# Last chunk of a two-layer mixture-of-experts kernel: half of its experts scaled by ScalarE and summed by TensorE with an identity; 6 buffers for expert values and 5 for fetched ones

## The chip, the core and the metric

The kernel runs on one core of one Trainium2 chip. A core has a matrix engine (TensorE, PE in the profile), a vector engine (VectorE, DVE), a scalar engine (ScalarE, ACT), a general engine (GpSimd, POOL), which here mostly issues gathers, and SyncE (SP), which issues plain transfers. Each engine takes its instructions from its own queue, in order. The metric is the device time of one execution in microseconds (us), the median of several runs.

## What is computed

Input x is 4 x 1024 tokens of 256 numbers in float32. There are two layers; each adds a gated attention-like part and a gated mixture of 8 experts, of which every token uses the best 2. The change lies in the mixture of the second layer. Cut to what matters:

```python
logits = x @ router_w.T                       # 8 experts
probs = softmax(logits)
topk_vals, topk_idx = top_k(probs, 2)
topk_w = topk_vals / (topk_vals.sum(-1) + 1e-06)
expert_out = einsum('nh,eho->eno', x, expert_weights)   # 256 -> 256 for each expert
out = ((expert_out[topk] + probs[topk]) * topk_w).sum()
x = x + gb * out                              # gb: one row of 256 for each batch
```

## The kernel before, in words

The tokens are cut into 8 chunks (c = 0 to 7) of 4 batches x 128 tokens. Layer 0 fills the time up to about 640 us and is not touched. In layer 1 each chunk is normalised (`normal`), goes through a gated feed-forward part (`fast`), is normalised again, and is routed (`routed`, `shares`).

**Chunks 0 to 6 do the experts sparsely.** Chunks 0 to 3 form one group (`ga`), chunks 4 to 6 another (`gb`). The normalised rows of a group are stored to memory (`gb_rows`) and sorted by expert into blocks of 128: 39 blocks for `ga`, 31 for `gb`. For each block, `block` (L2142) fetches 128 rows with a gather on POOL (tile `xg`), transposes them on PE (L2176), copies them with ACT (`xT`, L2182), multiplies them by one expert's matrix on PE (`p_e`, L2193), copies the result with ACT from PE's accumulator into a buffer `y` (L2203), and stores it with SP to memory (`gb_y`, L2206). The room for `y` is 3 buffers. When all blocks of a group are stored, `combine` (L1408) fetches for each chunk and each batch the two values of every token: two gathers on POOL into one buffer `yg` (L330), whose room is 3 buffers (`yg2=3`), then one ACT instruction (L1433) and three of DVE (L1439, L1442, L1444), the last of which adds to the tokens `x_sb`. After four batches a chunk is stored by SP in one transfer of 512 KB (L2381). For `gb` there are 3 x 4 = 12 such combinations with 24 gathers.

**Chunk 7 does its experts densely** (`dense`, L2213), all 8 for all tokens, so that its routing needs no sorting. For each batch b and each pair of experts j (0 to 3), PE multiplies the batch's tokens by the pair's matrices (L2241; two matmuls into one buffer of 512 numbers, shown by the profile as 4 records), and DVE multiplies each half by the token's weight for this expert and adds it to a running sum (`step`; L2257 for expert 0, L2266 for the others). At the end of a batch `done` (L2284) multiplies the sum by the gate (L2286) and adds it to `x_sb` (L2287), and SP stores 128 KB (L2290). The buffer of a pair is one of 3 (`p1`); the running sums have 2 buffers (`step`).

**What sets the order.** The instructions of layer 1 are not written in their final order. Each piece of work is given to a planner (`class Plan`, L39) with its engine, an estimated cost in us, what it comes after, which buffers it holds (the room by kind stands in `room1`, L1373 on) and a rank. `run` (L61) plays the work through in its own time: whenever an engine is free, the ready piece with the lowest rank is begun if its buffers are free, and the order that comes out is what each engine's queue then holds. So a new room or a new cost can move any later piece. The ranks that matter here: blocks of `gb` 7.35 to 8.0 (L2352), combinations of `gb` from 7.89 on (L2377), dense matmuls 8.23 + 0.1 b + 0.02 j (L2271), DVE's work on their results 0.5 below that (L2280), `done` 8.23 + 0.1 b (L2292).

Of the kernel before, what the change touches and what calls it, by code (L numbers as in the profile page):

```python
# [12 lines left out]
ALU = mybir.AluOpType  # L13
# [6 lines left out]
P = 128  # L20
B, S, D = 4, 1024, 256
NC = S // P
KD = D // P
E = 8
# [113 lines left out]
def adaln_d2_kernel(  # L138
# [20 lines left out]
    nc = tc.nc  # L159
# [7 lines left out]
    ps_2 = ctx.enter_context(tc.tile_pool(name="ps_2", bufs=2, space=PSUM))  # L167
    ps_m = ctx.enter_context(tc.tile_pool(name="ps_m", bufs=3, space=PSUM))

    def psum(pool, shape, name):  # L170
        tag = {id(ps_1): "p1", id(ps_2): "p2", id(ps_m): "pm"}[id(pool)]
        t = pool.tile([P, 512], F32, tag=tag, name=name)
        n = 1
        for s in shape[1:]:
            n *= s
        v = t[: shape[0], :n]
        if len(shape) == 3:
            v = v.rearrange("p (a b) -> p a b", b=shape[2])
        return v
# [57 lines left out]
    ident = const.tile([P, P], F32, name="ident")  # L237
# [3 lines left out]
    rank = const.tile([P, E], F32, name="rank")  # L241
# [600 lines left out]
    plan = Plan(p1=3, p2=2, pm=3, xn1=5, h1T=2, xn2=6, h2T=2, t1=1)  # L842
    PE, ACT, DVE, POOL = "PE", "ACT", "DVE", "POOL"
# [397 lines left out]
    ps = plan.slot("p1")  # L1241
# [27 lines left out]
    for half in range(2):  # L1269
        ps = plan.slot("p1")  # L1270
# [11 lines left out]
        m = plan(PE, 0.3, turn, after=routes, holds=[ps], rank=rank_)  # L1282
# [6 lines left out]
    for piece in range(3):  # L1289
        ps = plan.slot("p2")  # L1290
        m = loaded
        for k in range(KD):
# [12 lines left out]
            m = plan(PE, 0.87, mm, after=[m, of_batch["routed"]], holds=[ps], rank=20.0)  # L1305
# [5 lines left out]
    ps = plan.slot("p1")  # L1311
    d = of_batch["turned"]
    m = plan(PE, 0.2, lambda: g0.total_staged(ps_1), after=[d], holds=[ps], rank=-1.0)
    ps2 = plan.slot("p1")

    def bases():
# [3 lines left out]
    d = plan(DVE, 3.9, lambda: g0.close_staged(pa), after=[m], holds=[ps], rank=-1.0)  # L1320
# [4 lines left out]
        after=[m2],  # L1325
        holds=[ps2],
        rank=-0.9,
    )
    ps = plan.slot("p1")
    m = plan(PE, 0.4, lambda: g0.across(ps_1), after=[d], holds=[ps], rank=-1.0)  # L1330
    kept_busy(1.1, [m], 30.0)
    d = plan(DVE, 1.4, lambda: g0.limits(pa), after=[m, bs], holds=[ps], rank=-1.0)
    plan(DVE, 1.2, lambda: g0.list_weights(pa), after=[d], holds=[ps], rank=-0.75)
    for j in range(AHEAD):
        ps = plan.slot("p1")
# [12 lines left out]
        m = plan(PE, 0.25, look, after=[r], holds=[ps], rank=first)  # L1348
# [20 lines left out]
    for j in range(g0.J - SPARE, g0.J):  # L1369
# [6 lines left out]
        p2=2,  # L1376
        pm=3,
        yg1=3,
        yg2=3,
        h1=2,  # L1380
        h2=2,
        hT1=2,
# [1 line left out]
        hf=10,  # L1384
        xg=4,
        xT=3,
        y=3,
        reached=3,
        diff=2,
        step=2,  # L1390
# [6 lines left out]
    made = {}  # L1397
    home = {"yg1": early, "h1": early, "hT1": early, "tiny": early}

    def buf(kind, shape):  # L1400
        return (home[kind] if kind in home else late).tile(
            shape, F32, tag=kind, name=kind, bufs=room1[kind]
        )

    def tiny(shape, tag, n=2, dt=F32):
        return home["tiny"].tile(shape, dt, tag=tag, name=tag, bufs=n)
# [279 lines left out]
    plan = Plan(rings=RINGS, **room1)  # L1686
# [178 lines left out]
    plan = Plan(rings=RINGS, **room1)  # L1865
# [199 lines left out]
    def shares(g, c, at, vb, x, rank):  # L2065

        key = ("m", c)

        def do():
            x = made[key, "x"]  # L2070
            down = tiny([P, B, E + 1], "rdown")
            nc.vector.tensor_scalar(down, x, -1.0, 1.0, ALU.mult, ALU.add)
            nc.vector.reciprocal(down, down)
            nc.vector.scalar_tensor_tensor(x, x, 1.0, down, ALU.add, ALU.mult)
            p = tiny([P, 2, B], "rp")
            nc.vector.tensor_reduce(p[:, 0, :], x[:, :, :E], AX.X, ALU.add)
            nc.vector.reciprocal(p[:, 0, :], p[:, 0, :])
            nc.vector.tensor_tensor(
                p[:, 1, :].unsqueeze(2), x[:, :, E : E + 1], p[:, 0, :].unsqueeze(2), ALU.mult
            )  # L2080
            total = tiny([P, B], "rtotal")
            nc.vector.scalar_tensor_tensor(
                total, p[:, 0, :], 1e-6, p[:, 1, :], ALU.add, ALU.add
            )
            nc.vector.reciprocal(total, total)
            w = g.w[:, :, at : at + B]
            nc.vector.tensor_tensor(
                w, p, total.unsqueeze(1).to_broadcast([P, 2, B]), ALU.mult
            )
            nc.vector.tensor_tensor(p, p, w, ALU.mult)  # L2090
            nc.vector.tensor_tensor(vb[:, at : at + B], p[:, 0, :], p[:, 1, :], ALU.add)

        return plan(DVE, 2.2, do, after=[x[0]], holds=[x[1]], rank=rank)
# [119 lines left out]
    def dense(c, slotT, ts, d, x, rank):  # L2213

        key = ("d", c)
        g = last_pairs
        vb = tiny([P, B], "d_vb", 1)
        x = shares(g, c, 0, vb, x, rank)

        def spread_w():  # L2220
            w = made[key, "w"] = tiny([P, B, E], "d_w", 1)
            v = tiny([P, B, E], "d_v", 1)
            for i, t in ((0, w), (1, v)):
                nc.vector.tensor_tensor(
                    t,
                    g.one[:, i, :, :],
                    g.w[:, i, :].unsqueeze(2).to_broadcast([P, B, E]),
                    ALU.mult,
                )
            nc.vector.tensor_tensor(w, w, v, ALU.add)  # L2230

        x = plan(DVE, 0.6, spread_w, after=[x, d], rank=rank)
        for b in range(B):
            last, st = [], plan.slot("step")
            for j in range(E // 2):
                ps = plan.slot("p1")

                def mm(b=b, j=j):
                    p1 = made[key, b, j] = psum(ps_1, [P, 2, D], "p1_e")
                    for k in range(KD):  # L2240
                        nc.tensor.matmul(  # L2241
                            p1,
                            lhsT=made["n2", c, "hT"][:, k, b, :],
                            rhs=ew[:, 2 * j : 2 * j + 2, k, :],
                            start=(k == 0),
                            stop=(k == KD - 1),
                        )

                def out_(b=b, j=j):
                    if j == 0:  # L2250
                        made[key, "sum", b] = tiny([P, D], "step")
                    w, sum_ = made[key, "w"], made[key, "sum", b]
                    for i in range(2):
                        e = 2 * j + i
                        p = made[key, b, j][:, i, :]
                        if e == 0:
                            nc.vector.tensor_scalar(  # L2257
                                sum_,
                                p,
                                w[:, b, e : e + 1],  # L2260
                                vb[:, b : b + 1],
                                ALU.mult,
                                ALU.add,
                            )
                        else:
                            nc.vector.scalar_tensor_tensor(  # L2266
                                sum_, p, w[:, b, e : e + 1], sum_, ALU.mult, ALU.add
                            )

                m = plan(  # L2270
                    PE, 1.74, mm, after=ts, holds=[ps, slotT], rank=rank + 0.1 * b + 0.02 * j  # L2271
                )
                last = [
                    plan(
                        DVE,
                        0.95,
                        out_,
                        after=[m, x, *last],
                        holds=[ps, st],
                        rank=rank + 0.1 * b + 0.02 * j - 0.5,  # L2280
                    )
                ]

            def done(b=b):  # L2284
                sum_, xs = made[key, "sum", b], x_sb[:, c, b, :]
                nc.vector.tensor_tensor(sum_, sum_, mods1[GB][:, b, :], ALU.mult)  # L2286
                nc.vector.tensor_tensor(xs, xs, sum_, ALU.add)  # L2287

            def store(b=b):
                nc.sync.dma_start(out[b, c * P : (c + 1) * P, :], x_sb[:, c, b, :])  # L2290

            f = plan(DVE, 0.9, done, after=last, holds=[st], rank=rank + 0.1 * b)  # L2292
            plan(SP, 0.1, store, after=[f], rank=rank)

    last_pairs = Pairs(l1, l1, "gc", B)
# [8 lines left out]
    for c in range(NC):  # L2304
# [26 lines left out]
        if c == NC - 1:  # L2331
            d, x = routed(last_pairs, c, 0, slotT, ts, 7.46)
            dense(c, slotT, ts, d, x, 8.23)
            continue
        g, first = groups[which], 4 * which
        at = (c - first) * B
        d, x = routed(g, c, at, slotT, ts, c + 1.05)
# [12 lines left out]
        if c in (3, 6):  # L2350
# [15 lines left out]
            for q in range(first, c + 1):  # L2366
                done = combine(
                    "c2",
                    q,
                    "yg2",  # L2370
                    y_of[which],
                    g,
                    lambda b, q=q, first=first: (q - first) * B + b,
                    vbs[which],
                    mods1[GB],
# [70 lines left out]
```

## Time and profile before

| what | us |
|---|---|
| median of 3 runs (1152.88 to 1153.03) | 1153.02 |
| profiled execution, its own time | 1154.62 |
| span of the profiled execution | 1152.6 |
| PE busy in the span | 1100.8 (96%) |
| DVE, ACT, POOL busy | 586.6, 425.1, 410.6 |
| first gather of the last 12 combinations begins (POOL) | 1109.01 |
| last DVE instruction begins | 1148.23 |

The profile is one execution seen from inside. A line of a timeline gives the start, the length, the engine, the line of the kernel, the operation with output and input tiles, the number of instructions, and in brackets how long the engine had been idle before and what released it. A line of the groups gives count, busy time, and mean duration in ns. "Granted clock" is the share of TensorE's clock that its throttle let through.

A table of the last stretches, from the view of busy time by stretch:

| stretch, us | PE | DVE | ACT | POOL | granted clock |
|---|---|---|---|---|---|
| 1080 to 1095 | 13.83 of 15 | 7.38 | 7.79 | 9.55 | 1.00 |
| 1095 to 1105 | 8.84 of 10 | 3.78 | 4.74 | 1.58 | 1.00 |
| 1105 to 1115 | 10.00 of 10 | 6.05 | 1.57 | 4.72 | 1.00 |
| 1115 to 1125 | 10.00 of 10 | 8.31 | 2.12 | 7.61 | 1.00 |
| 1125 to 1135 | 6.33 of 10 | 6.74 | 1.17 | 4.24 | 1.00 |
| 1135 to 1142 | 3.63 of 7 | 6.22 | 1.51 | 4.33 | 0.76 |

### The profile page before, as it was taken

What the parts mean: (1) busy time and instruction counts of PE and PEld (TensorE: products, weight loads), DVE (VectorE), ACT (ScalarE), POOL (GpSimd) and SP (SyncE); (2) the same over time, 40 slices, a digit from 0 to 9 for tenths busy, and PEclk for the clock granted to TensorE, in tenths of its full rate; (3) what the DMA queues carried; (4) which work ended last, traced back from release to release, by engine and by line L of the source; (5) the groups of instructions that cost most, each with busy time, mean ns of one, the idle gap of its engine ahead of it and who ended that gap; (6) DMA issues with size and microseconds to landing.
All of it is one profiled execution on the core that took longest, in us unless ns stands there. A gap on an engine that the chain in (4) does not pass through costs nothing. (4 is left out here: it accounts for less than half of the span.)

```text
span 1152.6 us, 18406 instructions
## 1 busy us (share of the span) xinstructions
PE 1100.8 (96%) x6236; PEld 872.3 (76%) x6236; DVE 586.6 (51%) x2245; ACT 425.1 (37%) x1148; POOL 410.6 (36%) x477
## 2 busy tenths in 40 slices
PE   8999999999999999999989989999999999999893
PEld 5996899999999999999978455675667676646751
DVE  7777233222222212222245589878587535787566
ACT  5975333233333323233324433423324325342421
POOL 1000444333443344333463452420124332644644
PEclk8999999999999999999998999999999999999997
DMA  9412514564522415151251211200013323342544
GB/s 320 163 54 92 178 50 147 192 220 151 188 78 75 156 33 193 37 188 38 74 197 46 66 55 52 62 29 18 1 38 104 112 71 97 102 127 86 147 108 130
DMA packets 79369, 123.18 MB, mean 107 GB/s; under 512 B 23646, under 2 KB 63076, under 8 KB 74668
## 3 DMA queue, kind: packets, MB, share of 16 engines
q0 software_dynamic: 31680, 69.61, 19.9%
q1 hardware_dynamic: 46492, 50.80, 13.3%
q10 hardware_dynamic: 1104, 1.58, 0.4%
q8 instruction: 52, 0.85, 0.3%
q14 instruction: 41, 0.34, 0.1%
HBM read 205.18 MB, written 30.58 MB: 205 GB/s over the span
## 5 line engine op out<-in xcount | busy, mean ns | idle before, releaser
L1599 ACT ACTIVATE hid<-p_h,w 128x128 f32<-128x128 f32 x544 | 155.1, 368 | 338.0 <-issue 257.1
L1587 PEld LDWEIGHTS p_h<-xT,w 128*128 128x128 f32 x2176 | 255.4, 193 | 7.8 <-DVE xT L1572 4.0
L1587 PE MATMUL p_h<-xT,w 128*128 128x128 f32 x2176 | 257.1, 277 | 3.8 <-DVE xT L1572 3.2
L1610 PE MATMUL p_y<-w,hid 128*128 128x256 f32 x1088 | 251.6, 384 | 3.2 <-issue 3.2
L1884 PE MATMUL p_u<-hT,a 128*128 128x512 f32 x512 | 230.7, 595 | 0.8 <-ACTq L1848 0.8
L330 POOL DMA_INDIRECT w<-in_W,g_wrow x134 | 133.7, 998 | 271.6 <-ACT hid L1599 129.9
L1610 PEld LDWEIGHTS p_y<-w,hid 128*128 128x128 f32 x1088 | 202.6, 191 | 29.2 <-issue 4.2
L1884 PEld LDWEIGHTS p_u<-hT,a 128*128 128x128 f32 x512 | 94.2, 190 | 97.2 <-issue 89.3
L1572 DVE COPY xT<-pm_x 128x256 f32<-128x256 f32 x68 | 28.8, 424 | 186.8 <-PE pm_x L1567 176.4
L1932 PE MATMUL p_f<-a,hf 128*128 128x256 f32 x512 | 116.8, 380 | 3.9 <-DVE ln_mv L1467 1.6
L1621 DVE TENSOR_TENSOR y<-p_y,w 128x256 f32<-128x256 f32 x68 | 28.8, 424 | 176.1 <-PE p_y L1610 176.1
L1932 PEld LDWEIGHTS p_f<-a,hf 128*128 128x128 f32 x512 | 95.9, 190 | 22.6 <-issue 5.7
L330 POOL DMA_INDIRECT xg<-h_rows,g_row x68 | 65.7, 966 | 123.7 <-DVE g_hits L734 103.3
L330 POOL DMA_INDIRECT yg<-y,g_slot x64 | 61.4, 959 | 86.7 <-DVE x_sb L1444 33.5
L2193 PE MATMUL p_e<-ew,xT 128*128 x280 | 70.4, 384 | 0.3 <-ACT y L2203 0.3
L330 POOL DMA_INDIRECT xg<-ga_rows,ga_row x39 | 37.2, 954 | 91.3 <-DVE ga_row L743 35.0
L1896 ACT ACTIVATE hf<-p_u,decay 128x512 f32<-128x512 f32 x56 | 38.0, 683 | 72.6 <-PE p_u L1884 68.5
L2193 PEld LDWEIGHTS p_e<-ew,xT 128*128 128x128 f32 x280 | 49.4, 190 | 10.6 <-issue 5.1
L1507 DVE TENSOR_TENSOR h<-h,mod 128x256 f32<-128x256 f32 x128 | 51.5, 425 | 9.2 <-ACT h L1497 6.3
L1900 DVE SCALAR_TENSOR_TENSOR hf<-p_u,decay,hf 128x512 f32<-128x512 f32 x56 | 41.9, 748 | 21.8 <-PE p_u L1884 14.5
L2203 ACT COPY y<-p_e 128x256 f32<-128x256 f32 x70 | 26.0, 371 | 57.1 <-PE p_e L2193 24.8
L1980 POOL TENSOR_TENSOR x_sb<-x_sb,step 128x256 f32<-128x256 f32 x32 | 23.7, 743 | 62.2 <-DVE step L1973 44.5
(363 smaller groups left out, 1283.6 us busy)
## 6 DMA issues: line engine op xcount, KB each, us to landing
y<-y SPq DMA_DIRECT2D x68, 128.0 KB
ga_y<-y SPq DMA_DIRECT2D x39, 128.0 KB
x_sb<-in_x SPq DMA_DIRECT2D x8, 512.0 KB
h_rows<-xn SPq DMA_DIRECT2D x8, 512.0 KB
gb_y<-y SPq DMA_DIRECT2D x31, 128.0 KB
out_x<-x_sb SPq DMA_DIRECT2D x7, 512.0 KB
a<-in_fw SPq DMA_DIRECT2D x6, 512.0 KB
mod<-mod_rows SPq DMA_DIRECT2D x6, 512.0 KB
```

Source lines behind the costliest of these rows:

```text
L330: return nc.gpsimd.indirect_dma_start(out=dst, out_offset=None, in_=table, in_offset=bass.IndirectOffsetOnAxis(ap=index, axis=0), bounds_c ...
L1507: nc.vector.tensor_tensor(h, h, mods1[(sc, sh)[i]][:, b, :], (ALU.mult, ALU.add)[i])
L1572: nc.vector.tensor_copy(xT, pt)
L1587: nc.tensor.matmul(p1[:, i, :], lhsT=w1[:, k * H + m * P : k * H + (m + 1) * P], rhs=xT[:, k, :], start=(k == 0), stop=(k == KD - 1),)
L1599: nc.scalar.activation(hid[:, m, :], p1[:, i, :], AF.Relu, bias=w1buf[j % 2][:, KD * H + m : KD * H + m + 1],)
L1610: nc.tensor.matmul(p2, lhsT=hid[:, m, :], rhs=w2[:, m * D : (m + 1) * D], start=(m == 0), stop=(m == KH - 1),)
L1621: nc.vector.tensor_tensor(y, p2, w2buf[j % 2][:, KH * D :], ALU.add)
L1884: nc.tensor.matmul(pu, lhsT=a[:, k, m * P : (m + 1) * P], rhs=made["n1", c, "hT"][:, k, :, :], start=(k == 0), stop=(k == KD - 1),)
L1896: nc.scalar.activation(made[key, m], made[key, m, 0], AF.Silu, scale=decays[c])
L1900: nc.vector.scalar_tensor_tensor(h, made[key, m, 1], decays[c], h, ALU.mult, ALU.mult)
L1932: nc.tensor.matmul(made[key, "p2", b], lhsT=made[key, m][:, b * P : (b + 1) * P], rhs=a1[:, m, :], start=(m == 0), stop=(m == KH - 1),)
L2193: nc.tensor.matmul(made[key, "p2"], lhsT=made[key, "xT"][:, k, :], rhs=ew_flat[:, bass.ds(made[key, "at"] + k * D, D)], start=(k == 0), st ...
```

## The change

In `dense`, pairs j = 0 and 1 (experts 0 to 3) stay as they were. For pairs j = 2 and 3, ACT multiplies each half by the token's weight into a buffer of the kind `hf` (10 of them, free in this part of the kernel), and PE adds the two scaled halves into an accumulator `p2` by a matmul with the identity; four such matmuls make the batch's second sum. `done` adds that sum to DVE's running sum before the gate, so it has three instructions instead of two, and it waits for PE's last addition as well. Each batch holds one of the two `p2` buffers from its first addition to its `done`. The room for `yg2` grows from 3 to 5 and that for `y` from 3 to 6; both are used by group `ga` as well. Nothing else in the text of the kernel changes; the planner orders the whole of layer 1 anew from these entries.

```diff
@@ -1376,7 +1376,7 @@
         p2=2,
         pm=3,
         yg1=3,
-        yg2=3,
+        yg2=5,
         h1=2,
         h2=2,
         hT1=2,
@@ -1384,7 +1384,7 @@
         hf=10,
         xg=4,
         xT=3,
-        y=3,
+        y=6,
         reached=3,
         diff=2,
         step=2,
@@ -2232,6 +2232,8 @@
         x = plan(DVE, 0.6, spread_w, after=[x, d], rank=rank)
         for b in range(B):
             last, st = [], plan.slot("step")
+
+            half, summed, whole = E // 4, [], plan.slot("p2")
             for j in range(E // 2):
                 ps = plan.slot("p1")
 
@@ -2267,29 +2269,73 @@
                                 sum_, p, w[:, b, e : e + 1], sum_, ALU.mult, ALU.add
                             )
 
+                def scaled(b=b, j=j):
+                    t = made[key, "sc", b, j] = buf("hf", [P, 4 * P]).rearrange(
+                        "p (i d) -> p i d", i=2
+                    )
+                    for i in range(2):
+                        e = 2 * j + i
+                        nc.scalar.mul(
+                            t[:, i, :], made[key, b, j][:, i, :], made[key, "w"][:, b, e : e + 1]
+                        )
+
+                def add(b=b, j=j, half=half):
+                    if j == half:
+                        made[key, "p2", b] = psum(ps_2, [P, D], "p2_d")
+                    for i in range(2):
+                        nc.tensor.matmul(
+                            made[key, "p2", b],
+                            lhsT=ident,
+                            rhs=made[key, "sc", b, j][:, i, :],
+                            start=(j == half and i == 0),
+                            stop=(j == E // 2 - 1 and i == 1),
+                        )
+
                 m = plan(
                     PE, 1.74, mm, after=ts, holds=[ps, slotT], rank=rank + 0.1 * b + 0.02 * j
                 )
-                last = [
-                    plan(
-                        DVE,
-                        0.95,
-                        out_,
-                        after=[m, x, *last],
-                        holds=[ps, st],
-                        rank=rank + 0.1 * b + 0.02 * j - 0.5,
+                if j < half:
+                    last = [
+                        plan(
+                            DVE,
+                            0.95,
+                            out_,
+                            after=[m, x, *last],
+                            holds=[ps, st],
+                            rank=rank + 0.1 * b + 0.02 * j - 0.5,
+                        )
+                    ]
+                else:
+                    sc = plan.slot("hf")
+                    a = plan(
+                        ACT,
+                        0.9,
+                        scaled,
+                        after=[m, x],
+                        holds=[ps, sc],
+                        rank=rank + 0.1 * b + 0.02 * j - 0.4,
                     )
-                ]
+                    summed = [
+                        plan(
+                            PE,
+                            0.87,
+                            add,
+                            after=[a, *summed],
+                            holds=[sc, whole],
+                            rank=rank + 0.1 * b + 0.02 * j,
+                        )
+                    ]
 
             def done(b=b):
                 sum_, xs = made[key, "sum", b], x_sb[:, c, b, :]
+                nc.vector.tensor_tensor(sum_, sum_, made[key, "p2", b], ALU.add)
                 nc.vector.tensor_tensor(sum_, sum_, mods1[GB][:, b, :], ALU.mult)
                 nc.vector.tensor_tensor(xs, xs, sum_, ALU.add)
 
             def store(b=b):
                 nc.sync.dma_start(out[b, c * P : (c + 1) * P, :], x_sb[:, c, b, :])
 
-            f = plan(DVE, 0.9, done, after=last, holds=[st], rank=rank + 0.1 * b)
+            f = plan(DVE, 1.35, done, after=[*last, *summed], holds=[st, whole], rank=rank + 0.1 * b)
             plan(SP, 0.1, store, after=[f], rank=rank)
 
     last_pairs = Pairs(l1, l1, "gc", B)
```

## The prediction

> **What bounds the kernel now.** I read the page first (PE is busy for 96% of the span), then busy time by stretch. Up to about 1105 us PE is full or nearly so, and what moves there costs or gains little; from 1125 on PE has 6.33 of 10 us and then 3.63 of 7, so another thing ends the run. The chain of waits over the last stretch says which:
>
> ```profile
> 1140.37 0.94 POOL yg L330
> 1141.32 0.31 issue
> 1141.62 0.99 POOL yg L330
> ...
> 1144.23 2.93 DMA yg<-gb_y,gb_slot
> ...
> 1147.26 0.50 DVE yg L1439
> ```
>
> The end is the last of 24 gathers on POOL (1144.23), its landing, and three DVE instructions; after the last of these (1148.23, 0.43 long, so 1148.66) 3.94 us follow for the last 512 KB store, to the span's end at 1152.6. So I read POOL's timeline for the idle time before each gather:
>
> ```profile
> 1125.74 0.95 POOL L330 DMA_INDIRECT yg<-gb_y,gb_slot  x1 [0.30 <-issue]
> 1131.53 0.94 POOL L330 DMA_INDIRECT yg<-gb_y,gb_slot  x1 [4.84 <-DVE x_sb L1444]
> ...
> 1140.37 0.94 POOL L330 DMA_INDIRECT yg<-gb_y,gb_slot  x1 [1.45 <-DVE x_sb L1444]
> 1141.62 0.99 POOL L330 DMA_INDIRECT yg<-gb_y,gb_slot  x1 [0.31 <-issue]
> 1142.98 0.94 POOL L330 DMA_INDIRECT yg<-gb_y,gb_slot  x1 [0.37 <-DVE x_sb L1444]
> ```
>
> Between gathers lie 0.30 us when nothing is short. Three times it is 4.84, 1.45 and 0.37, and the releaser is DVE's last instruction of a combination (L1444): POOL waits for one of the 3 buffers. And DVE is late because it also adds up the dense experts:
>
> ```profile
> 1121.46 0.54 DVE L2257 TENSOR_SCALAR step<-p_e,d_w,d_vb 128x256 f32<-128x256 f32 x1
> ...
> 1123.41 0.42 DVE L1444 TENSOR_TENSOR x_sb<-x_sb,yg 128x256 f32<-128x256 f32 x1
> 1126.78 1.00 DVE L2266 SCALAR_TENSOR_TENSOR step<-p_e,d_w,step 128x256 f32<-128x256 f32 x2 [2.95 <-PE p_e L2241]
> 1128.95 1.00 DVE L2266 SCALAR_TENSOR_TENSOR step<-p_e,d_w,step 128x256 f32<-128x256 f32 x2 [1.16 <-remote]
> ```
>
> The 2.95 and 1.16 us are put down to PE and to "remote", though the first of these two pairs, the tenth in PE's order, had ended by about 1122; I can't explain them from the rows. In the 42.9 us from DVE's first dense instruction (1105.76) to 1148.66, DVE waits 7.7 us (1.52, 0.71, 0.71, 2.95, 1.16, 0.29, 0.33) and works 35.2.
>
> **The change part by part.**
>
> *DVE.* Two of four pairs of each batch go: 8 pairs of 1.00 us (the "x2" rows) = 8.0. Added: one 256-wide addition per `done`, 4 x 0.46 (its neighbours L2286 to L2287 follow at 0.46) = 1.8. DVE's work falls from 35.2 to 29.0 us.
>
> *ACT.* 16 scalings of 128x256 from PE's accumulator by a per-token weight. The trace has none of this form. The nearest rows:
>
> ```profile
> L1431 ACT ACTIVATE yg<-yg,g_w 128x256 f32<-128x256 f32 x32 | 16.3, 509 | 60.4 <-DMA yg<-y,g_slot 47.0 <-DVE ga_vb L2091 4.1 <-DVE x_sb L1444 3.3
> L2203 ACT COPY y<-p_e 128x256 f32<-128x256 f32 x70 | 26.0, 371 | 57.1 <-PE p_e L2193 24.8 <-issue 23.6 <-ACT xT L2182 3.0
> L1433 ACT ACTIVATE yg<-yg,gb_vb,gb_w 128x256 f32<-128x256 f32 x12 | 7.2, 600 | 32.3 <-DMA yg<-gb_y,gb_slot 23.4 <-DVE yg L1439 5.6 <-issue 3.2
> ```
>
> So 0.37 (same source, no weight) to 0.60 (weight and bias); I take 0.51, the scaling by a weight. 16 x 0.51 = 8.2 us, 1.02 a pair, where the planner reckons with 0.9. ACT has 1.6 to 2.1 of each 10 us in use there, so it is hidden; the wait it adds is the matter (below). The Trainium skill ("ScalarE: Activation LUTs", Rules for kernel authors) speaks against it: multiplications belong on VectorE. Here DVE's row is 0.48 to 0.50 a half and ACT's about the same, so the rule is right on speed, but DVE is the crowded engine; obeying it would leave DVE at 35.2 us and the gain at nearly nothing.
>
> *PE.* Eight additions of two 256-wide matmuls. A block's `p_e` (L2193) is the same shape, two matmuls shown as 4 records, 0.87 us. 8 x 0.87 = 7.0. The 16 dense pairs take 1.73 each (11 in 19.05), 27.7. From the first pair (1103.84), with the last block's 0.87 in between, PE ends at 1103.84 + 0.87 + 27.7 + 7.0 = 1139.4 if it never waits. A batch's `done` (0.1 and 3 x 0.46) then ends at 1140.9; its 128 KB store takes no longer than the 3.94 of 512 KB: 1144.8. That lies before the gather chain's end, so PE's 7.0 us are hidden, with about 2 us to spare.
>
> *Waits.* A PE addition waits for ACT; behind it stands the next dense pair. The planner can set a pair between, 1.73 us, against 0.1 + 1.02 that the scaling needs, so the wait is nothing unless ACT itself stands before a scaling waiting for a gather. `done` waits for PE's last addition; behind it on DVE stand combinations. DVE has 37.1 us (to 1142.9, below) for 29.0 of work, so 8.1 of waiting are covered, as much as it waits now. The waits on `hf` (10 buffers) and `p2` (2, a batch's is free at its `done`) come to nothing while `done` is in time.
>
> *yg2 = 5.* A combination holds its buffer from its first gather to L1444: 7.0 us for the first (1109.01 to 1115.99), 11.9 for the worst (1119.33 to 1131.26). Two gathers come every 2.57 us, so 5 buffers cover 12.9. All three stalls go: 4.84 + 1.45 + 0.37 - 3 x 0.30 = 5.76. What is late next is POOL's own pace. Without the relief of DVE the same buffers would give little: 35.2 of work and 7.7 of waits end where they end now. The two parts need each other.
>
> *y = 6.* Here ACT's copies wait for a store to free a buffer; PE's `p_e` buffers wait for them. In sight on PE:
>
> ```profile
> PE p_f L1932 <- ACT y L2203: 0.8, 1, 0.8
> ```
>
> (0.76 at 1059.61). In the order, the first dense pair (1103.84 to 1105.56) stands ahead of the last block, which sets the first gather. If free `y` buffers let the planner put the block first, that is 1.72 more. On the other side, a reshuffled order may put one more pair ahead: 1.72 lost. I take the 0.76, the one wait whose releaser is `y`; bounds -1.72 to +2.5. The same rooms for group `ga` move work around while PE is 97 to 100% busy (700 to 1040 us, in stretches of 50 to 100): I take nothing, and 1 us either way.
>
> SP issues the same stores and POOL the same gathers, in number and size.
>
> *Sum.* Last gather 1144.23 - 5.76 = 1138.47; to DVE 3.03 as now, 1141.50; three instructions 1.40, 1142.90; last store 3.94, 1146.84; less 0.76: 1146.1, against the span of 1152.6: 6.5 us. The profiled execution took 1154.62 itself, 2.0 above its span and 1.6 above the median of the runs; 6.5 off the median of 1153.02 gives **1146.5**.
>
> PE's clock bears on the end too: after a gap of 2.44 us the last dense pair took 3.63 us instead of 1.96, at a granted clock of 0.71 to 0.72. The skill ("TensorE: Matmul & The Clock Gate", What's actually happening) lets an idle window of 3.4 us halve the clock. With PE full to 1139 neither should happen; if it does, it costs 1.7 a pair and is within what PE has to spare.
>
> **Rivals.**
>
> 1. *The block stage gains too.* The last block goes ahead of the dense pair and the `y` waits go: 1146.84 - 0.76 - 1.72 = 1144.4, where PE's 1144.8 stops it. 1144.5 by the median's scale, at the best 1143.3. For: ACT waits twice for a `y` store after 1098 (2.0 us). Against: after 1098 the last blocks wait for rows (0.8 us on PE for `xg`), not for `y`.
> 2. *DVE and PE still hold each other up.* PE now loses 2.47 + 0.21 + 0.27 + 2.44 = 5.4 us waiting for DVE to empty its buffers. If that recurs, PE ends at 1144.8, and with 5.4 for `done` and store the span is 1150.2: 1150.6. For: the unexplained waits. Against: half of the buffers are now emptied by ACT.
> 3. *Slower: the scalings stand behind gathers.* ACT now waits 23.4 us in 10 waits for gathers to land, with nothing urgent behind. If a scaling is queued there, the PE addition and all dense pairs behind it wait. It decides from where PE's end passes 1154.9 - 5.4 = 1149.5, 10.1 us late, 1.26 for each of 8 additions. At 2.0 each PE ends at 1155.4 and the span at 1160.8: about 1161. Against: a gather reaches ACT after 2.83 us (1109.01 to 1111.84) and the planner reckons with 2.9, so plan and chip agree; only behind a 512 KB store was it 1.2 late (1124.49 to 1128.52).
> 4. *It doesn't do what it says*: the new order lets gathers begin late, or leaves `done` so late that the buffers fill all the same: 1153.
>
> **How the numbers follow.** Forecast (1145.0 to 1148.5) 0.58; rival 1 0.14; rival 2 0.14; rival 3 0.10; rival 4 0.04. Below 0.2%, 2.3 us, a measurement of this kernel can't tell a change from none: faster is under 1150.7. Forecast, rival 1 and two thirds of rival 2 are faster, 0.81; the rest of rival 2 and rival 4 the same, 0.09; rival 3 slower, 0.10. The range must reach rival 1's best, 1143.3, and most of rival 2, 1151.0; it leaves out rivals 3 and 4 and a little of 2.
>
> **What would show it.** Right: gathers from the first to the 24th 1.25 to 1.4 us apart with no wait over 0.5 for L1444; the last begins near 1138; ACT scalings 0.45 to 0.55; DVE idle 5 to 8 us after its first dense instruction; PE ends near 1139 to 1141 with its clock at 1.00. `y`: no wait of PE for ACT near 1059, and the last block before the first dense pair or not. Wrong: PE idle before its additions with ACT as releaser; POOL still waiting for L1444; the first gather after 1110; the order before 1040 costing more than 1 us.

## The result, and the profile after

The changed kernel took **1168.45 us** (median of 4 runs, 1164.67 to 1171.78) against 1153.03 (1152.88 to 1153.48, 4 runs) of the kernel before beside it: ratio 1.0132, 95% interval 1.0101 to 1.0163. It is slower by 15.4 us where 6.5 us less was predicted. Its profiled execution took 1168.73 with a span of 1167.0, 14.4 us more than before's span.

By stage, from POOL's timelines of the two kernels (us from the start of the span):

| | before | after | later by |
|---|---|---|---|
| first gather of `ga`'s combinations | 976.50 | 974.58 | -1.9 |
| first row gather of `gb`'s blocks | 1042.88 | 1049.08 | 6.2 |
| last row gather of `gb`'s blocks | 1095.94 | 1101.34 | 5.4 |
| first of the last 24 gathers | 1109.01 | 1116.91 | 7.9 |
| end of the span | 1152.6 | 1167.0 | 14.4 |

So there are three losses: 8.1 us between 975 and 1049 (from 1.9 ahead to 6.2 behind), 2.5 us between the last row gather and the first of the last 24 (15.6 where it was 13.1), and 6.5 us in the tail, which takes 50.1 us from its first gather where it took 43.6. Between the first two 0.8 us are won back.

POOL's timeline of the changed kernel, around the last long train of gathers of each group (start, length, engine, line, operation; in brackets the idle time before and what ended it):

```profile
989.64 0.95 POOL L330 DMA_INDIRECT yg<-ga_y,ga_slot  x1 [0.30 <-issue]
990.89 0.95 POOL L330 DMA_INDIRECT yg<-ga_y,ga_slot  x1 [0.30 <-issue]
999.22 0.94 POOL L330 DMA_INDIRECT yg<-ga_y,ga_slot  x1 [7.37 <-DVE x_sb L1444]
...
1139.68 0.95 POOL L330 DMA_INDIRECT yg<-gb_y,gb_slot  x1 [0.30 <-issue]
1140.94 0.95 POOL L330 DMA_INDIRECT yg<-gb_y,gb_slot  x1 [0.30 <-issue]
1150.16 0.95 POOL L330 DMA_INDIRECT yg<-gb_y,gb_slot  x1 [8.27 <-DVE x_sb L1444]
```

POOL runs 14 gathers on end in `ga` (before: 6, then 3.78 us for a buffer) and 20 in the tail (before: 14), and then stands 7.37 and 8.27 us for a buffer. The waits that the five buffers were to take away are larger, not gone. Who holds the buffers? DVE's timeline of the changed kernel:

```profile
987.68 0.42 DVE L1444 TENSOR_TENSOR x_sb<-x_sb,yg 128x256 f32<-128x256 f32 x1
993.83 0.75 DVE L1900 SCALAR_TENSOR_TENSOR hf<-p_u,decay,hf 128x512 f32<-128x512 f32 x1 [5.72 <-remote]
...
1129.66 0.42 DVE L1444 TENSOR_TENSOR x_sb<-x_sb,yg 128x256 f32<-128x256 f32 x1
1134.65 0.48 DVE L1439 SCALAR_TENSOR_TENSOR yg<-yg,gb_w 128x256 f32<-128x256 f32 x1 [4.57 <-issue]
...
1135.63 0.42 DVE L1444 TENSOR_TENSOR x_sb<-x_sb,yg 128x256 f32<-128x256 f32 x1
1145.36 0.54 DVE L2259 TENSOR_SCALAR step<-p_e,d_w,d_vb 128x256 f32<-128x256 f32 x1 [9.31 <-remote]
```

"Remote" is the profile's word for a wait whose releaser it finds on no engine of the core. By the kernel's text L2259 needs the first pair of batch 2 from PE, the weights, which DVE itself had written by 1114.1, and a `step` buffer, which DVE itself had given back by 1126.3 (batch 0's `done`). What is left is PE's signal. PE's timeline of the changed kernel shows when that pair, the ninth, ran:

```profile
1129.31 1.88 PE L2243 MATMUL p_e<-ew,hT 128*128 128x512 f32 x4
1133.82 1.13 PE L2286 MATMUL p_d<-hf,ident 128*128 128x256 f32 x4 [2.64 <-issue]
1134.79 3.60 PE L2243 MATMUL p_e<-ew,hT 128*128 128x512 f32 x8
1146.57 3.47 PE L2243 MATMUL p_e<-ew,hT 128*128 128x512 f32 x4 [8.18 <-DVE step L2268]
```

The pair had ended by 1131.2; DVE began on it at 1145.36, 14 us later. I call this a **late signal**. ACT has them too, as its timeline shows:

```profile
1133.30 0.84 ACT L2278 ACTIVATE hf<-p_e,d_w 128x256 f32<-128x256 f32 x2 [4.78 <-issue]
...
1145.56 0.84 ACT L2278 ACTIVATE hf<-p_e,d_w 128x256 f32<-128x256 f32 x2 [9.90 <-remote]
```

The first of these is the eighth pair, which PE had ended by about 1128.5; the profile calls the wait "issue", its word for a wait in which it sees nothing. PE's 2.64 and DVE's 4.57 us above come behind it. Once DVE is late, PE has no free buffer for the next pair and stands 8.18 us, POOL gets no `yg` buffer, and all three go on within a few us of each other. The chain that ended last goes through the same hole:

```profile
1136.05 9.32 another core or an unknown queue
...
1146.57 3.47 PE p_e L2243 x4
...
1153.48 5.15 PE p_e L2243 x12
```

The new operations cost little. From the groups of instructions of the changed kernel since 1100 (count, busy us, mean ns, idle time before):

```profile
L2286 PE MATMUL p_d<-hf,ident 128*128 128x256 f32 x32 | 8.2, 382 | 2.6 <-issue 2.6
...
L2278 ACT ACTIVATE hf<-p_e,d_w 128x256 f32<-128x256 f32 x16 | 6.7, 468 | 28.1 <-PE p_e L2243 13.4 <-remote 9.9 <-issue 4.8
```

16 scalings keep ACT busy for 6.7 us, 0.84 a pair, and an addition of two halves follows its neighbour on PE after 0.86.

### The profile page after: what moved, and what is told of

The parts are those of the page before. It is cut to its first block, busy times and chain, and to the rows that moved or that the text cites. A ratio compares the mean times of both kernels' runs of the same rounds, so it can differ in the third digit from the quotient of the medians.

```text
span 1167.0 us, 18436 instructions
## 1 busy us (share of the span) xinstructions
PE 1109.3 (95%) x6268; PEld 880.6 (75%) x6268; DVE 581.7 (50%) x2233; ACT 430.8 (37%) x1164; POOL 411.6 (35%) x477
## 3 DMA queue, kind: packets, MB, share of 16 engines
q1 hardware_dynamic: 46492, 50.80, 13.1%
## 5 line engine op out<-in xcount | busy, mean ns | idle before, releaser
L1900 DVE SCALAR_TENSOR_TENSOR hf<-p_u,decay,hf 128x512 f32<-128x512 f32 x56 | 41.9, 748 | 29.4 <-PE p_u L1884 15.5
```

The costliest lines, as they stand in the source:

```text
L1900: nc.vector.scalar_tensor_tensor(h, made[key, m, 1], decays[c], h, ALU.mult, ALU.mult)
```

## The experiments

**Two theories** at the start. *Train*: a long unbroken train of gathers on POOL goes with late signals from PE to DVE and ACT; the change makes the trains longer (6 to 14, 14 to 20), so it makes the signals later. Its rival, *order*: the time is lost because the planner's new order starts the dense matmuls 9.1 us later (1112.98 against 1103.84), or because the additions and scalings cost more than DVE gains. Two more came up with the runs: *occasion*, that late signals belong to some chips or occasions and not to others, and *split*, that they come from the new scalings and additions.

### Taking the change apart

Four kernels beside each other (each edit in one line): the change with `yg2` at 3; before with `yg2` at 5; the change with both rooms at 3 (the split of the last chunk alone); before with `y` at 6.

```diff
 e1_yg3 (from after)         -        yg2=5,   +        yg2=3,
 e2_before_yg5 (from before) -        yg2=3,   +        yg2=5,
 e3_split_only (from after)  -  yg2=5, y=6,    +  yg2=3, y=3,
 e4_before_y6 (from before)  -        y=3,     +        y=6,
```

> The changed kernel with 3 buffers for fetched values instead of 5 (dense half and 6 y buffers kept). Theory train: in the changed kernel's trace 14 gathers (974.58 to 991.84) and 20 gathers (1116.91 to 1141.89) follow each other without a pause, and DVE and ACT then wait 4 to 10 us for PE results that were ready long before, until shortly after the train ends; with 3 buffers POOL pauses after 6 to 14 gathers, so most of that goes: 1148 to 1155 us, and little spread between runs. Rival order: the time is lost because the planner's new order, from y=6 and the split, starts the dense matmuls 9.1 us later (1112.98 against 1103.84); then 3 buffers change little or hurt: 1160 to 1170.

> The kernel before with 5 buffers for fetched values and nothing else. Theory train: POOL runs 14 or more gathers on end for group ga and 20 for gb, PE loses 4 to 7 us before 1040 and the tail waits: 1158 to 1170 us, with spread. Rival order: without the split DVE stays the limit and the buffers do nothing: 1151 to 1154.

> Only the split of the last chunk's experts between DVE and ACT with PE (3 buffers for y and for fetched values as before). Theory train: nothing lengthens the trains of group ga, DVE is relieved by 6 us in the tail; 1148 to 1153. Rival order: the additions on PE and the scalings behind gathers on ACT cost more than DVE gains: 1156 to 1168.

> The kernel before with 6 buffers for y and nothing else. Theory train: the trains of gathers are as before; the y waits go: 1150 to 1154. Rival order: the new order of blocks and dense matmuls alone costs most of the 15 us: 1158 to 1168.

| kernel | us (range) | ratio to before | interval |
|---|---|---|---|
| before | 1138.79 (1135.79 to 1142.07) | | |
| e1_yg3 | 1137.47 (1135.49 to 1139.30) | 0.9989 | 0.9977 to 1.0001 |
| e2_before_yg5 | 1139.12 (1137.20 to 1142.46) | 1.0007 | 0.9994 to 1.0020 |
| e3_split_only | 1137.87 (1135.39 to 1139.61) | 0.9994 | 0.9981 to 1.0008 |
| e4_before_y6 | 1137.94 (1137.03 to 1140.79) | 0.9994 | 0.9979 to 1.0008 |

The times missed what either theory expected, and the reason is the first row: **before itself took 14 us less** than in the first comparison. None of the four traces has a wait marked remote, though e2 runs 19 gathers on end in `ga` and 24 in the tail. So a train alone makes no signal late, and no part of the change matters by more than 0.2% here. What was missing was the changed kernel on such an occasion, and these four on the other kind.

### The same two kernels again, and the change without y = 6

e5_changed_again and e6_before_again are the two kernels as they are; e7_without_y6 is the change with `y=3`.

> The changed kernel as it is, once more, beside new runs of the kernel before: in the first comparison before took 1153.0 us, in the second one, with four variants of it, 1138.8. Theory 'train' (the change itself makes the late signals: its unbroken trains of 14 and 20 gathers on POOL hold back what PE signals to DVE and ACT, on any occasion): ratio 1.010 to 1.016, so 1150 to 1157 us if before is at 1139, with waits marked remote of 4 us or more on DVE and ACT near the 14-gather train of combination ga and near the 20-gather train of the tail. Rival 'occasion' (the late signals belong to the occasion of the first comparison, in which before had some of them too, 1.2 to 5.1 us; what the change does to a chip without them is what its parts did): ratio 0.995 to 1.001, 1134 to 1140 us, no wait marked remote above 1 us.

> The kernel before as it is, for a profile of it on the occasion of the second and third comparisons. Theory 'train': its late signals follow from its own trains of at most 14 gathers, so its waits marked remote (5.1 us at 586 us, 1.2 us near 1129) come again at the same places, and the tail has POOL waits of 4.8 and 1.5 us for a buffer again. Rival 'occasion': span 1135 to 1140 us, no remote wait, the 4.8 us wait for a buffer gone and replaced by at most 1.5 us in all, since what held the buffer was the late signal.

> The changed kernel with y at 3 buffers in place of 6, so only the split of the last chunk and 5 buffers for fetched rows. Theory 'train': the tail keeps its 20-gather train and so its 8 us late signal, combination ga loses its 14-gather train; ratio 1.006 to 1.012. Rival 'occasion': ratio 0.995 to 1.001. By the prediction's own step for the tail alone (POOL's waits for a buffer go, whatever is left of them): 0.998 at the most where before has only 1 to 2 us of such waits left.

Before took 1154.09 us (1151.0 to 1156.68, 11 runs) this time. The changed kernel took 1166.72, ratio **1.0106** (1.0086 to 1.0127); without y = 6 it took 1164.17, 1.0085 (1.0062 to 1.0108). The late waits came again at the places of the first traces: in the changed kernel on DVE 5.77 us until 993.17 and 5.67 until 1143.22, on ACT 6.23 until 1134.78 and 6.33 until 1143.42; in before on DVE 5.10 until 586.58 and 3.93 until 1129.14, and POOL's wait for a buffer with 4.72 and 1.44 us. Without y = 6 the trains are nearly as long (14 and 18; the 14 of `ga` was expected to go) and the waits as late (9.68 us on DVE until 1139.04), and the two intervals overlap: y = 6 isn't the main cause. That the late waits stood at the same places, twice, spoke for *train*, and that before was back at 1154 for *occasion*; both seemed to be needed.

### The changed kernel on an occasion without late signals

e8_changed_third is the changed kernel, e9_yg3_again and e10_before_yg5_again are e1 and e2 once more, and e11_paced_tail breaks the tail's train in three places (shortened; `rest` is a spare tile of 128x256):

```diff
                     gather(made[key, c, b][:, i, :], y, g.slot[:, i, s : s + 1])
+                    n = (c - 4) * 2 * B + 2 * b + i + 1
+                    if kind == "yg2" and n in (6, 12, 18):
+                        for _ in range(10):
+                            nc.gpsimd.memset(rest, 0.0)
```

> The changed kernel as it is, beside the three variants below and new runs of before on the same occasion, since before took 1153 and 1154 us on two occasions and 1139 us on a third. Theory 'train and occasion' (on an occasion of the first kind, before at about 1154, signals of PE reach DVE and ACT late behind a long unbroken train of gathers; on one of the second kind, before at about 1139, they don't): ratio 1.009 to 1.014 if before is at 1150 or more, 0.995 to 1.001 if it is at 1142 or less. Rival 'the change is slow everywhere': ratio 1.009 to 1.014 at either.

> The changed kernel with 3 buffers for fetched rows in place of 5, so that POOL has to stop in its trains for a buffer: longest train 16 in the tail and 6 in combination ga on the occasion where before took 1139. Theory 'train': on an occasion of the first kind most of what the change costs goes with the 5 buffers, ratio 0.996 to 1.004, and the late waits near 994 us (4 to 6 us) are gone. Rival 'split' (the late waits come from the new scalings and additions themselves): ratio 1.008 or more. On an occasion of the second kind: 0.997 to 1.001, as it was.

> The kernel before with 5 buffers for fetched rows and nothing else. The prediction's own step for the buffers alone gives 0.995 to 0.999, since POOL's 4.8 and 1.4 us waits for a buffer go. Theory 'train': on an occasion of the first kind slower, 1.003 to 1.012, with a train of 19 gathers near 970 to 992 us and of 20 or more in the tail, and a late wait of 4 us or more near each one's end. Rival 'split': 0.995 to 1.000 at either kind, since there is no split in it. On an occasion of the second kind: 0.999 to 1.002, as it was.

> The changed kernel whose last 24 gathers are broken by three pauses of about 3 us on POOL (ten fills of a spare tile after the 6th, 12th and 18th). POOL's last gather can't issue before 1117 + 24 x 1.25 + 9 = 1156 us, against 1155 in the changed kernel. Theory 'train': on an occasion of the first kind the waits of 8 to 10 us of DVE, ACT and PE in the tail fall to under 4 us, and the time is within 4 us of the changed kernel's, since POOL takes over as the bound. Rival 'split': the long waits stay and the pauses add to them, changed + 6 to 9 us. On an occasion of the second kind both give changed + 6 to 9 us, since POOL sets the end there.

| kernel | us (range) | ratio to before | interval |
|---|---|---|---|
| before | 1137.47 (1135.33 to 1141.08) | | |
| e8_changed_third | 1136.67 (1133.62 to 1138.26) | 0.9989 | 0.9979 to 0.9998 |
| e9_yg3_again | 1135.83 (1134.99 to 1137.11) | 0.9984 | 0.9974 to 0.9993 |
| e10_before_yg5_again | 1137.91 (1136.23 to 1140.42) | 1.0005 | 0.9994 to 1.0016 |
| e11_paced_tail | 1146.77 (1144.93 to 1148.49) | 1.0076 | 1.0055 to 1.0096 |

The changed kernel isn't slow everywhere: the rival of e8 falls. On this occasion its tail does what the prediction said it would. POOL's timeline of e8_changed_third, the first and the last two of 24 gathers:

```profile
1095.26 0.95 POOL L330 DMA_INDIRECT yg<-gb_y,gb_slot  x1 [11.57 <-DMA gb_y<-y]
...
1123.38 0.95 POOL L330 DMA_INDIRECT yg<-gb_y,gb_slot  x1 [0.30 <-DVE x_sb L2333]
1124.63 1.14 POOL L330 DMA_INDIRECT yg<-gb_y,gb_slot  x1 [0.30 <-issue]
```

No wait between them exceeds 0.31 us, and the last begins 29.4 us after the first (35.2 in before's first trace; 29.5 was predicted, 1138.47 - 1109.01). PE runs its 16 pairs and 8 additions from 1092.71 to 1127.25 without a gap, and its last rows are at the full clock:

```profile
1120.21 5.31 PE L2243 MATMUL p_e<-ew,hT 128*128 128x512 f32 x12
1125.36 1.89 PE L2286 MATMUL p_d<-hf,ident 128*128 128x256 f32 x8
```

Then why only 0.1%? Because before has almost nothing to lose there. POOL's timeline of e4_before_y6, the kernel before but for `y`, on the occasion of the first experiments:

```profile
1115.54 0.94 POOL L330 DMA_INDIRECT yg<-gb_y,gb_slot  x1 [0.73 <-DVE x_sb L1444]
...
1124.38 0.94 POOL L330 DMA_INDIRECT yg<-gb_y,gb_slot  x1 [1.45 <-DVE x_sb L1444]
```

These are its only two waits for a buffer in the tail: 0.73 + 1.45 - 2 x 0.30 = 1.6 us, where before's first trace had 5.76 by the same sum. The 4.84 us wait was the trace of a late signal.

The paced tail shows that POOL's train sets the end here. POOL's timeline of e11_paced_tail at the first of the three pauses:

```profile
1102.87 0.95 POOL L330 DMA_INDIRECT yg<-gb_y,gb_slot  x1 [0.30 <-issue]
1103.81 3.65 POOL L1426 MEMSET rest<- 128x256 f32 x10
1107.61 1.10 POOL L330 DMA_INDIRECT yg<-gb_y,gb_slot  x1 [0.15 <-issue]
```

A pause adds some 3.5 us, three make 10.5, and the time rose by 10.1 (1146.77 - 1136.67), nearly all of it, and a little over the 6 to 9 expected, since a pause was meant to be 3 us.

### The question left: which part, on an occasion with late signals

e9, e10 and e11 had to run on an occasion of the other kind. They ran on four more occasions: e12_yg3_third, e15_yg3_fourth and e17_yg3_fifth are e9; e13_before_yg5_third, e16_before_yg5_fourth and e18_before_yg5_fifth are e10; e14_paced_again is e11.

> The changed kernel with 3 buffers for fetched rows, once more, for an occasion on which before takes 1150 us or more. Theory 'train' (late signals behind long unbroken trains of gathers, and the 5 buffers make the trains long): ratio 0.996 to 1.004, no late wait near 994 us, longest train of the tail under 16. Rival 'split' (late signals from the scalings and additions): 1.008 or more. If before takes under 1142: 0.997 to 0.999, as it was twice.

> The kernel before with 5 buffers for fetched rows, once more, for an occasion on which before takes 1150 us or more. Theory 'train': 1.003 to 1.012, a late wait of 4 us or more at the end of a train of some 14 to 19 gathers near 992 us, and one in the tail. Rival 'split': 0.995 to 1.000. If before takes under 1142: 1.000 to 1.001, as it was twice.

> The changed kernel with three pauses of 3 us in POOL's last 24 gathers, once more, for an occasion on which before takes 1150 us or more. Theory 'train': the waits of 8 to 10 us of DVE, ACT and PE in the tail fall to under 4 us and the time is within 4 us of the changed kernel's 1166.7 to 1168.5. Rival 'split': the waits stay, the time is 6 to 9 us above the changed kernel's. If before takes under 1142: ratio 1.007 to 1.009, as it was.

> The changed kernel with 3 buffers for fetched rows, for an occasion on which before takes 1150 us or more. Theory 'train': 0.996 to 1.004, no late wait near 994 us. Rival 'split': 1.008 or more. If before takes under 1142: 0.997 to 0.999, as it was three times.

> The kernel before with 5 buffers for fetched rows, for an occasion on which before takes 1150 us or more. Theory 'train': 1.003 to 1.012, with a late wait of 4 us or more near 992 us and one in the tail. Rival 'split': 0.995 to 1.000. If before takes under 1142: 1.000 to 1.001, as it was three times.

> The changed kernel with 3 buffers for fetched rows, for an occasion on which before takes 1150 us or more. Theory 'train': 0.996 to 1.004, no late wait near 994 us. Rival 'split': 1.008 or more. If before takes under 1142: 0.997 to 0.999, as it was four times.

> The kernel before with 5 buffers for fetched rows, for an occasion on which before takes 1150 us or more. Theory 'train': 1.003 to 1.012, with a late wait of 4 us or more near 992 us and one in the tail. Rival 'split': 0.995 to 1.000. If before takes under 1142: 1.000 to 1.001, as it was four times.

| kernel | before | us | ratio | interval |
|---|---|---|---|---|
| e12_yg3_third | 1138.02 | 1135.94 | 0.9987 | 0.9978 to 0.9996 |
| e13_before_yg5_third | 1138.02 | 1138.13 | 1.0002 | 0.9993 to 1.0011 |
| e14_paced_again | 1138.02 | 1146.57 | 1.0078 | 1.0062 to 1.0093 |
| e15_yg3_fourth | 1139.99 | 1137.66 | 0.9984 | 0.9971 to 0.9997 |
| e16_before_yg5_fourth | 1139.99 | 1138.92 | 0.9998 | 0.9986 to 1.0010 |
| e17_yg3_fifth | 1137.18 | 1136.31 | 0.9987 | 0.9973 to 1.0001 |
| **e18_before_yg5_fifth** | **1153.79** | **1166.39** | **1.0122** | 1.0097 to 1.0146 |

Three occasions had no late signals and gave the same numbers again. The last had them (before 1153.79, 1150.63 to 1155.79), and there **the two more `yg` buffers alone, with no scaling and no identity addition in the kernel, cost 1.22%**, as much as the whole change (1.06% and 1.32%). The prediction's step for the buffers said 0.995 to 0.999; *split* said 0.995 to 1.000; *train* said 1.003 to 1.012. POOL's timeline of e18_before_yg5_fifth:

```profile
989.97 0.95 POOL L330 DMA_INDIRECT yg<-ga_y,ga_slot  x1 [0.30 <-issue]
999.03 0.94 POOL L330 DMA_INDIRECT yg<-ga_y,ga_slot  x1 [8.11 <-DVE x_sb L1444]
...
1137.83 0.95 POOL L330 DMA_INDIRECT yg<-gb_y,gb_slot  x1 [0.30 <-issue]
1143.51 0.94 POOL L330 DMA_INDIRECT yg<-gb_y,gb_slot  x1 [4.74 <-DVE x_sb L1444]
```

The gather at 989.97 is the 14th on end, that at 1137.83 the 18th. DVE's timeline of the same run shows the late signals at the ends of the two trains:

```profile
993.65 0.75 DVE L1900 SCALAR_TENSOR_TENSOR hf<-p_u,decay,hf 128x512 f32<-128x512 f32 x1 [6.45 <-remote]
...
1140.93 1.00 DVE L2266 SCALAR_TENSOR_TENSOR step<-p_e,d_w,step 128x256 f32<-128x256 f32 x2 [6.02 <-remote]
```

The second of these is the eleventh pair of dense experts, the tenth of the eleven that PE ran in one piece from here:

```profile
1113.51 19.05 PE L2241 MATMUL p_e<-ew,hT 128*128 128x512 f32 x44
```

It ended at about 1113.51 + 10 x 1.73 = 1130.8, 10 us before DVE began on it. The same kernel on an occasion without late signals, e10_before_yg5_again, runs 19 gathers on end in `ga` and 24 in the tail; POOL's timeline:

```profile
990.80 1.01 POOL L330 DMA_INDIRECT yg<-ga_y,ga_slot  x1 [0.30 <-DVE yg L1439]
992.49 0.73 POOL L1980 TENSOR_TENSOR x_sb<-x_sb,step 128x256 f32<-128x256 f32 x1 [0.67 <-DVE step L1973]
995.71 0.96 POOL L330 DMA_INDIRECT yg<-ga_y,ga_slot  x1 [2.49 <-DVE x_sb L1444]
...
1125.19 1.00 POOL L330 DMA_INDIRECT yg<-gb_y,gb_slot  x1 [0.30 <-DVE step L2266]
1126.50 1.01 POOL L330 DMA_INDIRECT yg<-gb_y,gb_slot  x1 [0.30 <-issue]
```

and its DVE takes the corresponding L1900 with hardly a wait:

```profile
988.08 0.75 DVE L1900 SCALAR_TENSOR_TENSOR hf<-p_u,decay,hf 128x512 f32<-128x512 f32 x1 [0.46 <-PE p_u L1884]
```

Side by side (trains: gathers on end in `ga` and the tail; tail: from its first gather to the end of the span):

| kernel | signals late | trains | tail begins | tail lasts |
|---|---|---|---|---|
| before | yes | 6, 14 | 1109.0 | 43.6 |
| before, yg2 = 5 (e18) | yes | 14, 18 | 1116.1 | 47.7 |
| change without y = 6 (e7) | yes | 14, 18 | 1116.3 | 46.7 |
| change | yes | 14, 20 | 1116.9 | 50.1 |
| before, y = 6 (e4) | no | 6, 14 | 1097.1 | 39.5 |
| before, yg2 = 5 (e10) | no | 19, 24 | 1097.0 | 38.8 |
| split alone (e3) | no | 6, 16 | 1097.2 | 38.7 |
| change, yg2 = 3 (e9) | no | 6, 16 | 1096.7 | 38.4 |
| change (e8) | no | 19, 24 | 1095.3 | 38.6 |

**What is shown.** Two more `yg` buffers are enough for the whole slowdown (e18, four runs on one occasion), and only where signals are late. **What is argued.** That they do it through the longer trains. For it: nearly every remote wait over 1 us in the traces with late signals ends within 4 us after a train's last gather (one of 6.23 us, ACT's in e5, ends in the middle of one). Against it: late waits that the profile puts down to something else end inside trains too, such as ACT's 4.78 us in the changed kernel's first trace, 8.6 us before the train's end, and 2.99 us of DVE in e18 (until 1133.90, for a pair that had ended by about 1129.1), 4.9 us before it. The pauses of e11 never ran on such an occasion. And *order* isn't excluded there: the two buffers also change the planner's order, and no run with late signals has the one without the other. **What stays open.** Whether the change without the 5 buffers is faster, the same or slower there (it ran five times, and always where no signal was late); whether the chip or the occasion decides (the two chips on record with late signals had none of the other runs; one chip, twice used, had no late signals either time); and why a signal is late at all.

## Why the prediction was wrong

**What ends the run.** Right for before. In the changed kernel's first trace the chain of the tail goes through a late signal and then through PE's pairs and additions up to 1160.37, not through the gathers.

**"All three stalls go: 4.84 + 1.45 + 0.37 - 3 x 0.30 = 5.76."** This is the step that failed. It read a wait for a buffer as a shortage of buffers, and DVE's lateness as too much work. DVE gave the buffer back late because of a late signal: with 5 buffers the wait came back as 8.27 us (after), 8.02 (e5) and 4.74 (e18, the buffers alone). Without late signals, with all of the dense work still on DVE, the waits had been 1.6 us in all (e4). The sign was there: the 2.95 and 1.16 us of DVE that the prediction couldn't explain stand right ahead of the 4.84.

**"The same rooms for group `ga` move work around ...: I take nothing, and 1 us either way."** A second step that failed, by 8.1 us. e18 loses as much there (first gather of `ga` at 973.70, first row gather of `gb` at 1048.89: 75.2 us against before's 66.4) with the rooms of before but for `yg2`. A part of it is the new order alone: without late signals this stretch takes 68.7 to 70.6 us with 5 buffers (e2, e8, e10, e11, e13, e14, e16) and 66.0 to 66.3 with 3 (e1, e3, e4, e9, e12, e15, e17), and there the next stretch, to the last row gather, wins it back (46.2 to 47.1 us against 49.8 to 51.5). The rest comes only with late signals, and so does the loss of that gain (52.3 us in the changed kernel, 53.1 in before).

**DVE, ACT and PE.** The sizes held. A scaling takes 0.47, a pair 0.84 (predicted 0.51 and 1.02); an addition 0.86 to 0.87 (0.87); in e8 PE needs 34.5 us for all 16 pairs and 8 additions (34.7). ACT is as fast as DVE's 0.48 here, so the rule that the prediction weighed (the Trainium skill, "ScalarE: Activation LUTs", Rules for kernel authors: multiplications on VectorE) costs nothing to break for this shape. "The two parts need each other" wasn't borne out: without late signals neither is worth over 0.2%, alone (0.9994 and 1.0007) or together with y = 6 (0.9989).

**y = 6.** The last block does go ahead of the first dense pair (in the chain of the changed kernel PE's last three blocks run from 1110.55 to 1113.14, and the first pair follows), as rival 1 had it. Alone it gives 0.9994 (0.9979 to 1.0008), nothing that shows.

**PE's clock.** After the gap of 8.18 us the next pair took 3.47 us instead of 1.88. Busy time by stretch of the changed kernel (PE, PE's weight loads, DVE, ACT, POOL; then granted clock, share of DMA time, GB/s):

```profile
1130.00:1142.00 12.00, 5.75 (x15) 2.37 (x13) 1.42 (x4) 2.37 (x5) 9.14 (x10) 1.00 0.52 153
1142.00:1150.00 8.00, 3.43 (x5) 1.64 (x6) 4.43 (x11) 1.33 (x3) 0.00 (x0) 0.57 0.11 33
```

The clock is still 1.00 in the stretch in which PE falls idle, and 0.57 in the next. That agrees with the halving that the Trainium skill describes ("TensorE: Matmul & The Clock Gate", What's actually happening).

**The rivals.** Rival 2 ("DVE and PE still hold each other up. ... For: the unexplained waits") had the right place and the wrong size: it let PE's 5.4 us of waiting for DVE come again and priced that at 1150.6; PE lost 2.64 + 8.18 = 10.8 us in the tail alone, and 4.9 more in `ga` (30.1 of the 35 us from 975 to 1010, where before has all 35). Rival 3 ended on the right side by the wrong road: in e8, where no signal is late, PE has no gap ahead of an addition. In the changed kernel's first trace PE waits 2.64 us ahead of one, but for a scaling that stood behind a late signal, not behind a gather. Rival 1's sum is off by a little: 1144.4 of span is 1144.8 by the 0.4 us between span and median that the other sums use, not 1144.5, and no step gives its 1143.3. Rival 4's number, no change, is nearly what is left where no signal is late (0.1%), but not for its reasons: in e8 the gathers wait for no buffer.

## What to carry to other kernels

A wait for a buffer isn't a shortage of buffers until the holder's own delay is explained; a "remote" wait, or one put down to an engine that was long done, is the thing to explain first. More buffers let the engine that fills them run on unbroken and give the planner another order; here two more cost 1.22% on one kind of occasion, more than the wait they were to save. And before a difference of 1% is read, run the kernel before again on another chip: here before alone differed by 1.1 to 1.5% between occasions, and the change was 1.1 to 1.3% slower on one kind and 0.1% faster on the other.

## What the runs showed of the hardware that I had not expected

**Two kinds of occasion.** Before took 1153.0, 1154.1 and 1153.8 us in three comparisons and 1137.2 to 1140.0 in five, with the same program. In the first three DVE and ACT get PE's signals up to 14 us late. The loss of before is spread: its first `ga` gather begins at 976.50 against 966.5 to 970.0 in the variants on the other kind, its tail at 1109.0 against 1094.3 to 1101.5, and its span ends at 1152.6 against 1132.8 to 1140.2 (but for the paced tails).

**The record of semaphores is thinner there, too.** The traces with late signals hold 10,298 to 10,526 updates of semaphores, those without 14,284 to 14,335. It shows in the list of DMA issues, at the gathers. In e18_before_yg5_fifth the line of the last 24 has no time to landing:

```profile
yg<-gb_y,gb_slot POOLq DMA_INDIRECT x24
```

and for the same kernel in e10_before_yg5_again it has one:

```profile
yg<-gb_y,gb_slot POOLq DMA_INDIRECT x24, 2.8
```

All six traces with late signals lack the landing times of the gathers, and all fourteen without have them. The times of SP's stores don't tell: on the page they are missing in all six, but also in five of the fourteen (e1, e3, e9, e16, e17). So a list whose gathers have no landing times told, in these twenty traces, that the kernel ran on the kind with late signals, and before's list was such a one. Whether thin records and late signals have one cause isn't shown. The Trainium skill ("NOTIFIC — the notification-queue block", Overflow: three behaviours, one of which stalls the engine) describes a recording path that can hold an engine back; no run here shows whether that is at work.

**Prices.** Gathers of 128 rows of 256 numbers follow each other on POOL every 1.25 us (0.95 and 0.30) and land 2.9 us after issue (median of 24 in e2 and e4); a fill of 128x256 takes POOL 0.365 us.
